# Softmax of the first attention on ScalarE head by head, its tiles spread over the state recurrence, and the write term of the state chain added in the copy

## The chip, the core and the metric

The kernel runs on one core of one Trainium2 chip. The metric is device time of one execution in microseconds (us): the median of three runs before is 4936.85 us (4933.53 to 4939.53). Below, PE is TensorE, DVE is VectorE, ACT is ScalarE, POOL is GpSimd and SP is SyncE, whose queue issues the DMAs. Each engine works through its own instructions strictly in order.

## What is computed

The program is a stack of four blocks: an attention with a recurrent memory (called the first attention here), a six-layer local-attention model, a linear attention, and a two-layer local-attention model, each behind a modulated layer norm. Only the first attention is touched. Its reference, cut to what matters (B=4, T=512 in its own set-up; the kernel is called with 2 sequences of 2048 tokens, 16 heads of 8 dimensions, chunks of 64 tokens):

```python
def t_step(M, kv):
    k_t, v_t = kv
    Mk = jnp.einsum('bhde,bhe->bhd', M, k_t)
    forget = Mk[..., :, None] * k_t[..., None, :]
    write = v_t[..., :, None] * k_t[..., None, :]
    return (M - alpha * forget + beta * write, None)

def chunk_step(M, qkv):
    qi, ki, vi = qkv
    scores = jnp.einsum('bhid,bhjd->bhij', qi, ki) * scale
    scores = jnp.where(mask, -jnp.inf, scores)
    attn = jax.nn.softmax(scores, axis=-1)
    attn_out = jnp.einsum('bhij,bhjd->bhid', attn, vi)
    mem_out = jnp.einsum('bhid,bhde->bhie', qi, M)
    chunk_out = attn_out + 0.1 * mem_out
    M, _ = jax.lax.scan(t_step, M, kv)      # 64 steps
    return (M, chunk_out)
_, outs = jax.lax.scan(chunk_step, M0, (qc_all, kc_all, vc_all))   # 32 chunks
```

So every chunk has a causal softmax attention inside itself, and a 8x8 memory per head that is carried from chunk to chunk.

## The kernel before

The first attention is `l0_attention`. Its instruction order is written out by hand (`manual_schedule`): what the program emits first stands first on each engine, with semaphores put in by the framework where data, buffers or PSUM banks need them.

**Tiles.** The 4096 tokens make 32 tiles of 128 tokens (2 chunks). A tile's softmax weights are 128 rows x 16 heads x 64 keys: 1024 numbers per partition. The heads are split in two halves q of 8 heads, 512 numbers each, one PSUM bank per half. For one tile i:

- `spread(i)` (L390): POOL lays the keys out as block rows `kx`.
- `scores(i)` (L400): PE writes the causal mask (L405) and the scores (L411) into `ps_s`, one buffer of two banks.
- `shifted(i)` (L418): DVE takes the maximum of every row and head (L422), subtracts it (L424, PSUM to SBUF tile `sm`); ACT takes the exponential of all 1024 numbers at once (L425).
- `weights(i)` (L427): DVE sums them (L430) and takes the reciprocal (L431), POOL multiplies (L432).
- `keys_first(i)` (L434): PE transposes the weights (L440), ACT copies them out as `pT` (L444).
- `values(i)` (L446): PE projects the values into `ps_o` (L450), ACT copies them to `vbd` (L457).
- `mix(i, c)` (L462): PE multiplies weights and values for chunk c (L469), into the same banks of `ps_o`; ACT copies the result to `hT` (L476).

**The recurrence.** The memory's transition over a chunk does not depend on the memory itself, so all 64 chunks advance together: `step(t)` (L360) is called 64 times, each four DVE instructions (L366, L367, L369, L371) that depend on each other, and after every fourth step one ACT copy (L375). When the 64 steps are done, `products_done` sends the products through DRAM (`prd`) to lay them out anew.

**The chain over chunks.** Then `chain(n)` runs for n = 0 to 31, one after the other, for both sequences. PE multiplies the transition with the memory (L552) and adds the write term `rm` by a matmul with the identity into the same PSUM range (L557); DVE copies the sum out as the new memory `mn` (two copies of 64 partitions, L563); PE multiplies the old memory with the output weights (L567), and ACT copies that out as `xs` (L572, shown in the trace under the buffer name `bx`). `transitions(g)` prepares 8 chunks (L516, L530, L537), `turn_writes` turns the write terms (L498, L502), and `finish(g)` (`out_`, `centre`, `variance`, `scale`, L579 to L630) writes the output and the next layer norm for 1024 tokens.

**The main loop** (L675 to L699) weaves both. Iteration i emits `keys_first(i)`, `weights(i+1)`, `scores(i+2)`, `spread(i+3)`, `values(i+1)`, `shifted(i+2)`, `mix(i, 0)`, `mix(i, 1)`, and between them seven calls of `slot(i, part)`, which emit as many entries of the list `todo` as are due: 64 steps and `products_done` first (65 entries), then another 65: turning, transitions, chains and finishing. Which entries fall due when is one line (L670): the first 65 are spread over the tiles 0 to 25, the others over the tiles 26 to 31:

```python
due = 5 * q // 14 if i < 26 else 65 + (len(todo) - 65) * (q - 182) // 42
```

After the loop, `finish(3)` runs by itself, and the local models (`local_models`, untouched) start.

Of the kernel before, what the change touches and what calls it, by code (L numbers as in the profile page):

```python
# [72 lines left out]
def tile_kernel(ctx: ExitStack, tc: tile.TileContext, a: dict, out: bass.AP):  # L73
    nc = tc.nc
# [37 lines left out]
    identb = const.tile([128, 128], BF16, name="identb")  # L112
# [75 lines left out]
    def l0_attention(m):  # L188
# [17 lines left out]
        maskb = cp.tile([128, 8, 64], BF16, name="maskb")  # L206
# [22 lines left out]
        with tc.tile_pool(name="a_p", bufs=2) as wp, tc.tile_pool(  # L229
            name="a_psP", bufs=2, space=PSUM  # L230
# [101 lines left out]
        wk = ctx2.enter_context(tc.tile_pool(name="a_w", bufs=2))  # L332
        psS = ctx2.enter_context(tc.tile_pool(name="a_psS", bufs=1, space=PSUM))
# [26 lines left out]
        def step(t):  # L360
            full = (128, 8, 8, 8)
            kt = bc(kd[:, t].unsqueeze(2), full)
            four = zks[:, t // 4 % 2]
            zk = four[:, t % 4]
            tm = wk.tile([128, 8, 8, 8], F32, name="tm")
            nc.vector.tensor_tensor(tm, z, kt, ALU.mult)  # L366
            nc.vector.tensor_reduce(zk, tm, AX.X, ALU.add)  # L367
            up = wk.tile([128, 8, 8, 8], F32, name="up")
            nc.vector.tensor_tensor(up, bc(zk.unsqueeze(3), full), kt, ALU.mult)  # L369
            flat = lambda v: v.rearrange("p c r e -> p (c r e)")  # L370
            nc.vector.scalar_tensor_tensor(  # L371
                flat(z), flat(up), na[:, 0:1], flat(z), ALU.mult, ALU.add
            )
            if t % 4 == 0:
                nc.scalar.copy(  # L375
                    wr[:, :, :, t:t + 4], four.rearrange("p t c r -> p r c t")
                )
# [3 lines left out]
        for i in range(2):  # L381

            v = wk.tile([128, 2, 8, 72], F32, name=f"vbd{i}", bufs=1)
# [15 lines left out]

        def scores(i):  # L400
            t0 = 128 * order[i]
            kx = L[i].pop("kx")
            sp = L[i]["s"] = psS.tile([128, 1024], F32, name="ps_s")
            for q in range(2):
                nc.tensor.matmul(  # L405
                    sp[:, 512 * q:512 * q + 512], lhsT=identb,
                    rhs=maskb.rearrange("p h k -> p (h k)"), start=True, stop=False,
                )
            for c in range(2):
                for q in range(2):  # L410
                    nc.tensor.matmul(  # L411
                        sp[64 * c:64 * c + 64, 512 * q:512 * q + 512],
                        lhsT=qT[64 * q:64 * q + 64, t0 + 64 * c:t0 + 64 * c + 64],
                        rhs=kx[64 * q:64 * q + 64, c].rearrange("p h j -> p (h j)"),
                        start=False, stop=True,
                    )

        def shifted(i):  # L418

            v = L[i].pop("s").rearrange("p (q h k) -> p h q k", q=2, h=8)  # L420
            mx = wk.tile([128, 8, 2], F32, name="mx")
            nc.vector.tensor_reduce(mx, v, AX.X, ALU.max)  # L422
            sm = L[i]["p"] = wk.tile([128, 8, 2, 64], F32, name="sm", bufs=3)
            nc.vector.tensor_tensor(sm, v, bc(mx.unsqueeze(3), (128, 8, 2, 64)), ALU.subtract)  # L424
            nc.scalar.activation(sm, sm, AF.Exp)  # L425

        def weights(i):  # L427
            sm = L[i]["p"]
            rs = wk.tile([128, 8, 2], F32, name="rs")
            nc.vector.tensor_reduce(rs, sm, AX.X, ALU.add)  # L430
            nc.vector.reciprocal(rs, rs)  # L431
            nc.gpsimd.tensor_tensor(sm, sm, bc(rs.unsqueeze(3), (128, 8, 2, 64)), ALU.mult)  # L432

# [28 lines left out]
        def mix(i, c):  # L462
            t0 = 128 * order[i]
            vf = vbd[i % 2].rearrange("p c h x -> p c (h x)")
            pT = L[i]["pT"]
            for h in range(8):
                for q in range(2):
                    qs = slice(64 * q, 64 * q + 64)
                    nc.tensor.matmul(  # L469
                        po[qs, q, 0, i % 2, 64 * c:64 * c + 64],  # L470
                        lhsT=vf[qs, c, 64 * h:64 * h + 64],
                        rhs=pT[qs, h, 64 * c:64 * c + 64], start=(h == 0), stop=(h == 7),
                    )
# [6 lines left out]
        E = {}  # L480
        QS = [slice(0, 64), slice(64, 128)]
# [61 lines left out]
        def chain(n):  # L543
            c = n % 8
            pm = E["p"][:, :, 128 * (n % 2):128 * (n % 2) + 128].rearrange(
                "p q (b f) -> p q b f", b=2)
            px = E["p"][:, :, 256:512].rearrange("p q (b f) -> p q b f", b=2)
            if n < 31:
                for b in range(B):
                    for q in range(2):  # L550
                        if n:
                            nc.tensor.matmul(  # L552
                                pm[QS[q], q, b], lhsT=E["bd"][QS[q], b, c],
                                rhs=E["m"][QS[q], b], start=True, stop=False,
                            )
                    for q in range(2):
                        nc.tensor.matmul(  # L557
                            pm[QS[q], q, b], lhsT=ident[QS[q], QS[q]],
                            rhs=E["rm"][QS[q], c % 2, b, c // 2], start=(n == 0), stop=True,
                        )  # L560
                mn = wk.tile([128, 2, 64], F32, name="mn")
                for q in range(2):
                    nc.vector.tensor_copy(mn[QS[q]], pm[QS[q], q])  # L563
            if n:
                for b in range(B):
                    for q in range(2):
                        nc.tensor.matmul(  # L567
                            px[QS[q], q, b], lhsT=E["m"][QS[q], b], rhs=wo10[QS[q], :],
                            start=True, stop=True,
                        )  # L570
                for q in range(2):
                    nc.scalar.copy(E["xs"][QS[q], :, c, :], px[QS[q], q])  # L572
            if n < 31:
                E["m"] = mn
# [58 lines left out]
        def finish(g):  # L633
            bs = (g, NBLK + g)
            return [lambda f=f, k=k: f(k) for f in (out_, centre, variance, scale) for k in bs]
# [11 lines left out]
        todo = [lambda t=t: step(t) for t in reversed(range(64))]  # L647
# [16 lines left out]
        def slot(i, part):  # L664

            nonlocal done
            if i < 0:
                return
            q = 7 * i + part + 1
            due = 5 * q // 14 if i < 26 else 65 + (len(todo) - 65) * (q - 182) // 42  # L670
            while done < due:
                todo[done]()
                done += 1

        for i in range(-3, NT):  # L675
            if i >= 0:
                keys_first(i)
            if 0 <= i + 1 < NT:
                weights(i + 1)
            slot(i, 0)  # L680
            if 0 <= i + 2 < NT:
                scores(i + 2)
            slot(i, 1)
            if i + 3 < NT:
                spread(i + 3)
            if 0 <= i + 1 < NT:
                values(i + 1)
            slot(i, 2)
            if 0 <= i + 2 < NT:
                shifted(i + 2)  # L690
            slot(i, 3)
            if i >= 0:
                mix(i, 0)
                slot(i, 4)
                mix(i, 1)
            slot(i, 5)
            slot(i, 6)
            if i == -1:
                regroup()  # L699
# [843 lines left out]
    with ExitStack() as ctx2:  # L1543
        hs0 = l0_attention(m0)
# [65 lines left out]
```

## Time and profile before

| What | us |
|---|---|
| median of the three runs | 4936.85 |
| the profiled execution's own time | 4928.13 |
| its span (first to last instruction) | 4926.3 |
| PE busy in the span | 4493.8 (91%) |
| DVE busy in the span | 3949.1 (80%) |
| POOL busy | 2781.2 (56%) |
| ACT busy | 2637.9 (54%) |

How to read it: a share of busy time is a mean over stages with different limits. The first attention takes only the first part of the span: its tile loop begins at about 87 us, the last of the 64 steps starts at 381.9 us, the last chain matmul stands at about 550 us, and the first matmul of the local models (L871) at 566.6 us. The page's 40 slices are 123 us each, so the tile loop lies in slices 1 to 5; there PE shows 5 to 7 tenths and DVE 8 to 9 tenths in the slices that hold the steps. Everything after 566.6 us belongs to parts that the diff does not touch.

### The profile page before, as it was taken

The page shows a single profiled execution, that of the slowest core. Times are in us where ns is not written, and L with a number is a line of the kernel's source. Part 1 is how long each engine was busy: PE and PEld are TensorE (multiplying, and loading weights), DVE is VectorE, ACT ScalarE, POOL GpSimd, SP SyncE. Part 2 cuts the span into 40 slices and gives each one's busy share as a digit, 9 for nine tenths or more (in the row PEclk, how much of TensorE's full clock was granted, in tenths as well). Part 3 has the DMA queues.
Part 4 walks back from the last instruction along what each step waited for, and adds up shares of the span by engine and source line. Part 5 has one row for each costly group of instructions (what it writes and reads, how often), then busy time and mean ns, then how long its engine had stood idle before and what let it go on. Part 6 is the DMA issues. An engine that isn't in the chain of part 4 may idle for free.

```text
span 4926.3 us, 166334 instructions
## 1 busy us (share of the span) xinstructions
PE 4493.8 (91%) x73028; PEld 3066.5 (62%) x73058; DVE 3949.1 (80%) x6840; ACT 2637.9 (54%) x4207; POOL 2781.2 (56%) x1666
## 2 busy tenths in 40 slices
PE   5667799999999999999999999999999998899997
PEld 4445566666666666666666666666666665556554
DVE  6994488888888888888887888888877777788886
ACT  3223355555555555555555555555555555465554
POOL 3332366666666666666666666666655544455552
PEclk8778899999999999999999999999999999999999
DMA  2000222222222322223222322222212111111121
GB/s 78 1 1 25 85 65 67 69 73 70 69 65 64 87 68 65 66 73 76 68 64 64 79 72 65 66 74 69 68 51 59 50 51 46 37 46 49 51 58 41
DMA packets 222468, 295.31 MB, mean 60 GB/s; under 512 B 75657, under 2 KB 95409, under 8 KB 221745
## 3 DMA queue, kind: packets, MB, share of 16 engines
q1 hardware_dynamic: 221744, 284.67, 22.4%
q8 instruction: 576, 9.44, 0.8%
q14 instruction: 148, 1.20, 0.1%
HBM read 40.98 MB, written 10.75 MB: 10 GB/s over the span
## 4 chain that ended last, share of the span: by engine, by line
PE 49%; DVE 25%; ACT 7%; POOL 5%; issue 3%; DMA 0%; SPq 0%; POOLq 0%; DVEq 0%; ACTq 0%
PE ps_qk L871 12%; PE ps_o L1050 5%; PE ps_v L957 5%; DVE ps_qk L899 5%; PE ps_f L1150 5%; DVE t L888 5%; PE ps_turn L938 4%; PE ps_y L1067 4%; POOL r L894 4%; PE ps_s L997 3%; DVE r L883 3%; PE ps_fy L1175 3%; ACT sq L873 2%; DVE rs L1021 2%; PE ps_pT L1032 2%
## 5 line engine op out<-in xcount | busy, mean ns | idle before, releaser
L894 POOL TENSOR_TENSOR r<-r,t 128x1024 f32<-128x1024 f32 x448 | 1060.2, 2367 | 911.8 <-DVE t L888 794.3
L906 POOL TENSOR_TENSOR r<-r,rq_y 128x1024 f32<-128x1024 f32 x448 | 843.8, 1902 | 517.9 <-DVE rq_y L180 495.8
L873 ACT ACTIVATE sq<-ps_qk 128x1024 f32<-128x1024 f32 x448 | 460.6, 1028 | 1082.3 <-PE ps_qk L871 1014.7
L871 PE MATMUL ps_qk<-wp,hs 128*128 128x512 f32 x1792 | 893.8, 621 | 105.7 <-DVE rq_y L180 77.1
L883 DVE TENSOR_TENSOR r<-ps_qk,tb 128x1024 f32<-128x1024 f32 (+1 forms) x512 | 550.7, 1076 | 211.8 <-ACT sq L873 198.4
L1050 PEld LDWEIGHTS ps_o<-pT,v 64*64 64x64 f32 (+1 forms) x26624 | 479.4, 136 | 304.5 <-ACT pT L1033 160.9
L888 DVE TENSOR_TENSOR t<-ps_qk,tb 128x1024 f32<-128x1024 f32 (+1 forms) x512 | 554.1, 1082 | 143.1 <-POOL r L894 142.4
L1023 POOL TENSOR_TENSOR sm<-sm,rs 128x1024 f32<-128x1024 f32 x256 | 487.5, 1904 | 210.2 <-DVE rs L1022 126.9
L1050 PE MATMUL ps_o<-pT,v 64*64 64x32 f32 (+1 forms) x26624 | 531.2, 221 | 37.0 <-ACT pT L1033 19.2
L899 DVE TENSOR_REDUCE ps_qk<-sq 128x16 f32<-128x1024 f32 x448 | 549.0, 1226 | 11.9
L871 PEld LDWEIGHTS ps_qk<-wp,hs 128*128 128x128 f32 x1792 | 310.1, 193 | 364.3 <-issue 236.1
L938 PEld LDWEIGHTS ps_turn<-ident,r 128*128 128x128 f32 x3584 | 411.7, 143 | 125.2 <-issue 99.4
L957 PE MATMUL ps_v<-wp,hs 128*128 128x512 f32 x896 | 481.9, 639 | 1.0 <-ACT oT L1056 0.8
L1067 PEld LDWEIGHTS ps_y<-oT,wo 128*128 128x128 f32 x3584 | 430.2, 193 | 46.9 <-issue 42.5
L938 PE MATMUL ps_turn<-ident,r 128*128 128x128 f32 x3584 | 447.3, 277 | 9.7 <-POOL r L906 4.1
L1067 PE MATMUL ps_y<-oT,wo 128*128 128x128 f32 x3584 | 446.3, 276 | 1.5 <-ACT oT L1056 1.5
L1056 ACT COPY oT<-ps_o 128x512 f32<-128x512 f32 x448 | 244.0, 588 | 281.9 <-PE ps_o L1050 281.2
L1005 DVE TENSOR_REDUCE mx<-ps_s 128x16 f32<-128x1024 f32 (+1 forms) x256 | 312.5, 1221 | 97.4 <-PE ps_s L997 95.6
L997 PE MATMUL ps_s<-kT,qT 64*32 64x64 f32 (+1 forms) x26624 | 377.9, 230 | 0.7 <-issue 0.5
L997 PEld LDWEIGHTS ps_s<-kT,qT 64*32 64x32 f32 (+1 forms) x26624 | 325.8, 107 | 63.7 <-issue 53.0
L1150 PE MATMUL ps_f<-fx,w 128*128 128x512 f32 (+1 forms) x768 | 356.1, 600 | 2.5 <-DVE fx L1133 1.7
L1021 DVE TENSOR_REDUCE rs<-sm 128x16 f32<-128x1024 f32 (+1 forms) x256 | 310.5, 1213 | 51.1 <-ACT sm L1014 49.0
(265 smaller groups left out, 6850.5 us busy)
## 6 DMA issues: line engine op xcount, KB each, us to landing
v<-vn SPq DMA_DIRECT2D x1276, 128.0 KB
v<-vn SPq DMA_DIRECT2D x744, 64.0 KB
v<-vn SPq DMA_DIRECT2D x64, 256.0 KB
wp<-in_L_ffn_Wqkv SPq DMA_DIRECT2D x20, 512.0 KB
xD<-xb SPq DMA_DIRECT2D x24, 256.0 KB
xb<-xD SPq DMA_DIRECT2D x24, 256.0 KB
cs<-in_cos SPq DMA_DIRECT2D x128, 32.0 KB
cs<-in_sin SPq DMA_DIRECT2D x128, 32.0 KB
```

Of the source, the lines that this page charges most:

```text
L871: nc.tensor.matmul(pq[:, js], lhsT=hw, rhs=wts[g, u][:, js], start=True, stop=True)
L883: nc.vector.tensor_tensor(r[:, es].rearrange("p (h d) -> p h d", d=DH), pq[:, es].rearrange("p (h d) -> p h d", d=DH), bc(tb[:, 0, s].unsq ...
L888: nc.vector.tensor_tensor(t2[:, es].rearrange("p (h s d) -> p h s d", s=2, d=32), pq[:, es].rearrange("p (h s d) -> p h s d", s=2, d=32)[: ...
L894: nc.gpsimd.tensor_tensor(r, r, t2, ALU.add)
L899: nc.vector.tensor_reduce(pq[:, 16 * v:16 * v + 16], st[i].pop(("sq", v)).rearrange("p (h d) -> p h d", d=DH), AX.X, ALU.add,)
L906: nc.gpsimd.tensor_tensor(rv, rv, bc(y[:, 16 * v:16 * v + 16].unsqueeze(2), (128, 16, DH)), ALU.mult)
L938: nc.tensor.transpose(p[:, c * 128:(c + 1) * 128], r[:, cs], ident)
L957: nc.tensor.matmul(p, lhsT=hw, rhs=wv, start=True, stop=True)
L997: nc.tensor.matmul(sp[W * w:W * w + W, c0:c0 + 2 * W], lhsT=qT[64 * q:64 * q + 64, cc, W * w:W * w + W], rhs=kT[64 * q:64 * q + 64, cc, W ...
L1050: nc.tensor.matmul(po[s][64 * q:64 * q + 64, 128 * c + W * w:128 * c + W * w + W], lhsT=v2[kp, w, co:co + 64], rhs=pT[kp, q, c, W * w:W * ...
L1067: nc.tensor.matmul(py[:, 0:128], lhsT=wts[g, "o"][:, c * NO + s, :], rhs=oT[:, s, c, :], start=(c + s == 0), stop=(c == 3 and s == NO - 1),)
L1150: nc.tensor.matmul(ps_[c][0:sz], lhsT=wts[g, "w1"][:, o:o + sz], rhs=S["x"], start=True, stop=True,)
```

## The change

Four edits, all in `l0_attention`:

1. The scores' PSUM tile is split into two, one bank per half q, and the three matmuls of a half stand together.
2. `shifted` is replaced by `maxima` (two DVE maximum reductions of 512 numbers, negated) and `exps(i, q)`: eight ACT exponentials of 64 numbers for each half, straight from PSUM, with the negated maximum as the bias and the sum over the 64 numbers returned through the accumulator (`accum_out`) into `rs`. The subtraction on DVE (L424) and the sum on DVE (L430) are gone.
3. In the main loop `maxima(i+2)` and `exps(i+2, 0)` stand where `shifted(i+2)` stood, `exps(i+2, 1)` after `mix(i, 1)`. The first 65 entries of `todo` are spread over tiles 0 to 28, the other 65 over tiles 29 to 31.
4. In `chain` the identity matmuls (L557) are gone; the DVE copy that makes `mn` becomes an addition of PSUM and `rm`.

```diff
         def scores(i):
...
             for q in range(2):
+                sp = L[i]["s", q] = psS.tile([128, 8, 64], F32, name=f"ps_s{q}")
+                flat = sp.rearrange("p h k -> p (h k)")
                 nc.tensor.matmul(
-                    sp[:, 512 * q:512 * q + 512], lhsT=identb,
+                    flat, lhsT=identb, rhs=maskb.rearrange("p h k -> p (h k)"),
...
-        def shifted(i):
...
-            nc.vector.tensor_reduce(mx, v, AX.X, ALU.max)
-            sm = L[i]["p"] = wk.tile([128, 8, 2, 64], F32, name="sm", bufs=3)
-            nc.vector.tensor_tensor(sm, v, bc(mx.unsqueeze(3), (128, 8, 2, 64)), ALU.subtract)
-            nc.scalar.activation(sm, sm, AF.Exp)
+        def maxima(i):
+            mx = L[i]["mx"] = wk.tile([128, 8, 2], F32, name="mx")
+            for q in range(2):
+                nc.vector.tensor_reduce(mx[:, :, q], L[i]["s", q], AX.X, ALU.max, negate=True)
+
+        def exps(i, q):
...
+            sp, mx = L[i].pop(("s", q)), L[i]["mx"]
+            for h in range(8):
+                nc.scalar.activation(
+                    L[i]["p"][:, h, q, :], sp[:, h, :], AF.Exp, bias=mx[:, h, q:q + 1],
+                    accum_out=L[i]["rs"][:, h, q:q + 1],
+                )
 
         def weights(i):
-            sm = L[i]["p"]
-            rs = wk.tile([128, 8, 2], F32, name="rs")
-            nc.vector.tensor_reduce(rs, sm, AX.X, ALU.add)
+            sm, rs = L[i]["p"], L[i].pop("rs")
             nc.vector.reciprocal(rs, rs)
...
-                                rhs=E["m"][QS[q], b], start=True, stop=False,
+                                rhs=E["m"][QS[q], b], start=True, stop=True,
                             )
-                    for q in range(2):
-                        nc.tensor.matmul(
-                            pm[QS[q], q, b], lhsT=ident[QS[q], QS[q]],
-                            rhs=E["rm"][QS[q], c % 2, b, c // 2], start=(n == 0), stop=True,
-                        )
...
-                    nc.vector.tensor_copy(mn[QS[q]], pm[QS[q], q])
+                    r = E["rm"][QS[q], c % 2, :, c // 2]
+                    if n:
+                        nc.vector.tensor_tensor(mn[QS[q]], pm[QS[q], q], r, ALU.add)
+                    else:
+                        nc.vector.tensor_copy(mn[QS[q]], r)
...
-            due = 5 * q // 14 if i < 26 else 65 + (len(todo) - 65) * (q - 182) // 42
+            due = 65 * q // 203 if i < 29 else 65 + (len(todo) - 65) * (q - 203) // 21
...
-                shifted(i + 2)
+                maxima(i + 2)
+                exps(i + 2, 0)
             slot(i, 3)
             if i >= 0:
                 mix(i, 0)
                 slot(i, 4)
                 mix(i, 1)
+            if 0 <= i + 2 < NT:
+                exps(i + 2, 1)
```

More of the change, by code (lines that the diff above doesn't have):

```diff
@@ L402, in scores @@
             kx = L[i].pop("kx")
-            sp = L[i]["s"] = psS.tile([128, 1024], F32, name="ps_s")
             for q in range(2):
+                sp = L[i]["s", q] = psS.tile([128, 8, 64], F32, name=f"ps_s{q}")
+                flat = sp.rearrange("p h k -> p (h k)")
                 nc.tensor.matmul(
-                    sp[:, 512 * q:512 * q + 512], lhsT=identb,
-                    rhs=maskb.rearrange("p h k -> p (h k)"), start=True, stop=False,
-                )
-            for c in range(2):
-                for q in range(2):
+                    flat, lhsT=identb, rhs=maskb.rearrange("p h k -> p (h k)"),
+                    start=True, stop=False,
+                )
+                for c in range(2):
                     nc.tensor.matmul(
-                        sp[64 * c:64 * c + 64, 512 * q:512 * q + 512],
+                        flat[64 * c:64 * c + 64, :],
                         lhsT=qT[64 * q:64 * q + 64, t0 + 64 * c:t0 + 64 * c + 64],
@@ L416, in scores @@
                     )
-        def shifted(i):
-            v = L[i].pop("s").rearrange("p (q h k) -> p h q k", q=2, h=8)
-            mx = wk.tile([128, 8, 2], F32, name="mx")
-            nc.vector.tensor_reduce(mx, v, AX.X, ALU.max)
-            sm = L[i]["p"] = wk.tile([128, 8, 2, 64], F32, name="sm", bufs=3)
-            nc.vector.tensor_tensor(sm, v, bc(mx.unsqueeze(3), (128, 8, 2, 64)), ALU.subtract)
-            nc.scalar.activation(sm, sm, AF.Exp)
+        def maxima(i):
[3 more added lines that the diff above has]
+        def exps(i, q):
+            if q == 0:
+                L[i]["p"] = wk.tile([128, 8, 2, 64], F32, name="sm", bufs=3)
+                L[i]["rs"] = wk.tile([128, 8, 2], F32, name="rs")
+            sp, mx = L[i].pop(("s", q)), L[i]["mx"]
[4 more added lines that the diff above has]
+                )
         def weights(i):
-            sm = L[i]["p"]
-            rs = wk.tile([128, 8, 2], F32, name="rs")
-            nc.vector.tensor_reduce(rs, sm, AX.X, ALU.add)
+            sm, rs = L[i]["p"], L[i].pop("rs")
             nc.vector.reciprocal(rs, rs)
@@ L553, in chain @@
                                 pm[QS[q], q, b], lhsT=E["bd"][QS[q], b, c],
-                                rhs=E["m"][QS[q], b], start=True, stop=False,
+                                rhs=E["m"][QS[q], b], start=True, stop=True,
                             )
-                    for q in range(2):
-                        nc.tensor.matmul(
-                            pm[QS[q], q, b], lhsT=ident[QS[q], QS[q]],
-                            rhs=E["rm"][QS[q], c % 2, b, c // 2], start=(n == 0), stop=True,
-                        )
                 mn = wk.tile([128, 2, 64], F32, name="mn")
                 for q in range(2):
-                    nc.vector.tensor_copy(mn[QS[q]], pm[QS[q], q])
+                    r = E["rm"][QS[q], c % 2, :, c // 2]
[3 more added lines that the diff above has]
+                        nc.vector.tensor_copy(mn[QS[q]], r)
             if n:
```

## The prediction

> **What bounds the kernel now.** I first took the time line to place the tile loop, then the busy time by stretch. In the answer the columns are the stretch, its length, busy time of PE, PEld, DVE, ACT and POOL with instruction counts, granted clock, DMA share and GB/s.
>
> ```profile
> 102.40:384.80 282.40, 175.28 (x2325) 119.27 (x2349) 272.18 (x361) 89.08 (x200) 101.50 (x54) 0.76 0.00 1
> 384.80:553.00 168.20, 128.55 (x1740) 100.52 (x1740) 53.11 (x115) 57.23 (x128) 29.37 (x22) 0.86 0.08 25
> ```
>
> The first stretch holds tiles 0 to 25 and the 64 steps: DVE is busy 272 of 282 us, everyone else below two thirds. The second holds tiles 26 to 31 and the chains: PE leads with 129 of 168 us, DVE has 53. So one edit can pay in each stretch, and by a different engine. The groups by form show what a tile puts on DVE (last numbers: busy, mean ns | idle before).
>
> ```profile
> L371 DVE SCALAR_TENSOR_TENSOR z<-up,c_L_attn_a,z 128x512 f32<-128x512 f32 x64 | 48.4, 756 | 2.2
> L367 DVE TENSOR_REDUCE zks<-tm 128x64 f32<-128x512 f32 x64 | 44.5, 695 | 3.2
> L424 DVE TENSOR_TENSOR sm<-ps_s,mx 128x1024 f32<-128x1024 f32 x32 | 39.2, 1224 | 1.1
> L422 DVE TENSOR_REDUCE mx<-ps_s 128x16 f32<-128x1024 f32 x32 | 39.0, 1219 | 4.9 <-PE ps_s L411 4.8
> L430 DVE TENSOR_REDUCE rs<-sm 128x16 f32<-128x1024 f32 x32 | 38.8, 1214 | 2.4 <-ACT sm L425 2.4
> L431 DVE RECIPROCAL rs<-rs 128x16 f32<-128x16 f32 x32 | 8.1, 253 | 1.1
> ```
>
> A tile costs DVE 1.22 + 1.22 + 1.21 + 0.25 = 3.91 us. A step, from its start at 201.42 us to the next instruction's at 204.20, takes 2.78. With 64/26 = 2.46 steps a tile that is 10.75, against 282.4/26 = 10.86 measured: DVE is the bound, with no wait worth naming. For what ACT pays per small instruction I read its groups and one run of three in the time line (start, length):
>
> ```profile
> L444 ACT COPY pT<-ps_pT 128x512 f32<-128x512 f32 x64 | 35.0, 590 | 6.5 <-PE ps_pT L440 5.8
> L457 ACT COPY vbd<-ps_o 64x128 f32<-64x128 f32 x64 | 16.7, 261 | 12.6 <-PE ps_o L450 11.7
> L1160 ACT ACTIVATE u<-ps_f,c 128x512 f32<-128x512 f32 x128 | 82.1, 685 | 19.4 <-PE ps_f L1150 18.8
> L200 ACT ACTIVATE c_L_attn_a<-c_L_attn_a 128x1 f32<-128x1 f32 x1 | 0.2, 203 | 2.5 <-DMA c_L_attn_a<-in_L_attn_a 2.5
> 766.75 1.83 ACT L1160 ACTIVATE u<-ps_f,c 128x512 f32<-128x512 f32 x3
> ```
>
> Three activations with a bias column, 685 ns each, end within 1.83 us: one starts every (1.83 - 0.685)/2 = 0.57 us, an overlap of 0.11.
>
> **Part 1, exponential on ACT.** DVE loses L424 and L430 and has two maxima of 512 for one of 1024: 2 x 0.69 (L367's size) for 1.22. A tile falls from 3.91 to 1.63, and with 64/29 = 2.21 steps DVE's own work is 1.63 + 6.14 = 7.8 us.
>
> ACT gets 16 pairs of a 64-number exponential and an accumulator read for one 1.06 us exponential. The exponential: an element costs (590 - 261)/384 = 0.857 ns, so 448 fewer than L1160's take 0.38 off 0.57: 0.19 us start to start. The read has no row. Below: 0, if it hides in the exponential. Above: 0.203, ACT's smallest instruction (L200) unoverlapped, behind an exponential that doesn't overlap either (0.685 - 0.38 = 0.30): 0.50 a pair. I take the small instruction with the usual overlap, 0.203 - 0.11 = 0.09, as ACT's queue overlaps wherever no semaphore stands between, and none does here. A pair is 0.285, 16 are 4.56; the ends are 3.0 and 8.1.
>
> The Trainium skill speaks against sixteen small activations: "ScalarE: Activation LUTs", section "What ACT_TABLE_LOAD costs", gives 280 ns + 0.833 per element with a pointer bias and an overlap of 93, hence an estimate of 0.24 for 64 numbers where this trace's spacing gives 0.19; the sum below would be 16 x 0.05 x 29 = 23 us longer by it.
>
> ACT's total, 4.56 plus copies (two of 0.59, four of 0.26, 0.55 x 0.37 for L375: 2.4) is 7.0 us a tile, below DVE. But the two engines now wait for each other in a ring. The reciprocal of tile i+2 on DVE, at the head of the next iteration, waits for the last pair of `exps(i+2, 1)`; behind it are queued that iteration's steps and maxima. `exps` in turn waits for the maxima. One turn:
> - DVE from the last pair: semaphore 0.06, reciprocal 0.2, the one step that falls due in slots 0 to 2 (steps are 3.12 slots apart), 2.78, first maximum 0.69, semaphore 0.06: 3.8 us. Beside it PE does half 1's scores (L411, about 1.5) and the values (0.5), ACT `pT` (1.07) and `vbd` (0.55), some 3.2 us: hidden, with 0.6 to spare.
> - then ACT: 16 pairs 4.56, `hT` copies 0.56, last read's tail and semaphore 0.15, share of L375 0.1: 5.4 us. PE's mix (2.1 us at full clock, 3.6 at half) lies beside the first half. DVE does the second maximum and 1.25 steps here, 4 us, but where two steps fall due (28% of tiles) 6.1 us: mean 5.6.
>
> Turn: 9.4 us, with DVE idle some 1.6 of it. 29 tiles: 271 us. It starts later: tile 1's exponentials and the `kd` copies queue on ACT ahead of the first step: about 104 instead of 102.4, plus 1.9 as the `kd` copies (2 x 1.97) delay tile 0's `exps`. End of the steps: 104 + 1.9 + 271 = 377 instead of 384.8: **-8 us**, with three more tiles done.
>
> **Part 2, tail.** These groups of PE are from 385 to 553 us:
>
> ```profile
> L567 PE MATMUL ps_n<-wo,mn 64*64 64x128 f32 x248 | 23.6, 317 | 29.9 <-DVE mn L563 28.7 <-ACT bx L572 1.2
> L552 PE MATMUL ps_n<-mn,bx 64*64 64x64 f32 x240 | 18.6, 245 | 5.7 <-ACT bx L572 5.3 <-POOL bx L516 0.4
> L557 PE MATMUL ps_n<-rm,ident 64*64 64x64 f32 x248 | 18.2, 236 | 0.0
> L469 PE MATMUL ps_o<-pT,vbd 64*64 64x64 f32 x384 | 16.5, 242 | 0.0
> ```
>
> PE's in-order queue is the path: its busy 129 us and about 36 of waits, mostly 0.9 us behind every `mn` copy, make up the 168. Three tiles leave: 3 mixes of 16.5/6, 3 transposes of 8.2/5 (L440), 2 scores of 1.8 (L405 and L411), 3 values of 0.46: about **-18**. DVE loses some 14 us of tile work here, of which little stood ahead of an `mn`: -3. Covers that go: chains with nothing between them wait on the `xs` copy (0.9 us; L552 shows 5.3 in all). Some 11 such gaps instead of 6: +5. Tile 31's two blocks of 2.3 us on ACT stand in front of `xs` copies, where before four of 1.06 did: +2. `products_done` (8 DMAs, then the load of `pc`) moves from tile 25's end to tile 28's on SP, which is idle in both; the 12 us from there to the first L552 (384.8 to 397.06) were filled by turning, `rm`, scores and a mix, and lose part of that: +1. The 0.37 us ACT copies, POOL's `spread` and the output's loads keep their places.
>
> **Part 3, write term in the copy.** The two identity groups between L552's lie about 0.12 us each at full clock, 0.21 at half (535.08 us on): 0.24 to 0.42 x 31 = 7.4 to 13 us, on the path since `mn` waits for them. Adding from PSUM and SBUF is priced by L1073, the same shape (64x128): 286 ns, as L563's copy: nothing. I take **-8**, near the full-clock end, as the granted clock of that stretch is 0.86; `rm` comes from DVE itself and is ready long before.
>
> Tail: -18 - 3 + 5 + 2 + 1 - 8 = -21; I take **-19**, as PE's granted clock (0.86) may fall with more gaps. Sum: -8 - 19 = -27. On the profiled execution, 4928.13 us (span 4926.3, 1.8 around it), that is 4901; this one lay 8.7 below the median, so on 4936.85 it is **4910 us**.
>
> **Rivals.** *The read waits for its exponential.* If the accumulator can only be read when the exponential has drained, a pair costs 0.19 + 0.203 = 0.39, 16 are 6.3, the ring turns in 3.8 + 7.1 = 10.9 us and 29 tiles take 316: 45 more than I count, 4955 us, slower. It decides from 0.375 a pair upward; 0.35 is break-even (27/29 = 0.9 us a tile over 5.6). For it: every L425 waits on DVE at present, so ACT has shown no dependent pair back to back; L457's pairs, which wait by semaphore, don't overlap (0.55 for two). Against it: pairs carry no semaphore.
>
> *The read is free.* At 0.19 a pair ACT's part is 3.9, with the two-step tiles 4.5 in the mean, the turn 8.3, 29 tiles 240: 4879 us. DVE's 7.8 is the floor.
>
> *The tail does not shrink.* Chains keep their latency (matmul, copy, matmul, copy: about 2.9 us x 32 = 93), the output's loads their 3.2 us, so that what the three tiles leave turns into waits for `xs` and `mn`. Then only part 1 remains: 4929 us, no change. For it: 30 us of PE's idle before L567. Against: PE is busy 129 of 168.
>
> **How the numbers follow.** Forecast 0.48, its own range 4896 to 4926; slow read 0.25; free read 0.12; tail unchanged 0.15. A measurement here can tell about 0.2%, 10 us. Faster: 0.48 + 0.12 and a little of the third, 0.62; same 0.15; slower 0.23. Range 4879 to 4956: to the free read below and past the slow read above, leaving out the pair at 0.50 (12.7 us a turn, 5006).
>
> **What would show it.** Pairs on ACT 0.285 us apart; DVE idle about 1.6 us a tile in front of the reciprocal, released by ACT; tiles 9.4 us apart; the steps' end near 377 us; the tail some 149 us long, with L552 waiting more on `xs`. I am wrong if a pair takes over 0.35, if the steps' stretch shows ACT waiting for PE's scores, or if PE's idle in the tail grows by what its work shrinks.

## The result and the profile after

| | before | after |
|---|---|---|
| median, us | 4937.17 (8 runs, 4931.15 to 4940.96) | 4954.58 (8 runs, 4945.79 to 4959.94) |
| ratio after/before, 95% | | 1.0035 [1.0025, 1.0045] |
| profiled execution, us | 4928.13 | 4947.9 |
| its span | 4926.3 | 4946.1 |

The changed kernel is slower by 17.4 us. It was predicted faster by 27. The page's own line of busy time shows little of why:

```profile
PE 4547.7 (92%) x72809; PEld 3088.3 (62%) x72810; DVE 3876.8 (78%) x6808; ACT 2757.0 (56%) x5199; POOL 2780.7 (56%) x1666
```

DVE lost 72 us and ACT gained 119, as meant. But PE gained 54 us although the diff gives it fewer matmuls: 47.8 of them in the stretch of the steps, 6.4 in the tail. Busy time by stretch shows it. The columns are those of the prediction: stretch, length, busy time of PE, PEld, DVE, ACT and POOL, PE's granted clock, DMA share, GB/s. The first stretch runs to the end of the 64 steps (start of the copy `zs`). The second, the tail, runs from there to the first matmul of the local models, which need the whole of this attention. First the tail of the kernel before, with that boundary:

```profile
384.90:566.80 181.90, 139.80 (x1803) 110.03 (x1803) 57.02 (x123) 59.04 (x130) 31.39 (x24) 0.86 0.12 37
```

Then both stretches of the kernel after:

```profile
105.00:390.00 285.00, 220.56 (x2610) 137.14 (x2609) 216.48 (x343) 211.01 (x1144) 111.39 (x60) 0.81 0.01 2
390.00:579.40 189.40, 146.20 (x1295) 112.12 (x1295) 44.07 (x110) 54.38 (x143) 20.11 (x18) 0.68 0.11 35
```

In the stretch of the steps PE had 172.8 us in the kernel before (105 to 384.9 us); now there are three tiles more, and the scores take longer. Their rows, before and after:

```profile
L411 PE MATMUL ps_s<-kx,qT 64*64 64x512 f32 x212 | 40.1, 834 | 5.8 <-issue 3.5
L411 PE MATMUL ps_s<-kx,qT 64*64 64x512 f32 x232 | 71.1, 693 | 0.0
```

A tile's scores took 40.1/26.5 = 1.51 us and take 71.1/29 = 2.45. The kernel before emitted the matmuls of the two halves in turn, and its records overlap (212 of 834 ns in 40.1 us, 4.4 at a time); edit 1 puts each half by itself, and 2.3 overlap.

Three more things are to be seen. The steps end at 390.0 instead of 384.9 us: DVE is now busy 216 of 285 us, so it is no longer full, and ACT has 211. The tail is 7.5 us longer (189.4 against 181.9), with 508 fewer matmul records in it. And PE's busy time in the tail rose by 6.4 us, while its idle time is as before (43.2 against 42.1). So the lost time is in the matmuls themselves: the granted clock fell from 0.86 to 0.68. A *link* below is one call `chain(n)`: first product (transition times memory), copy `mn` on DVE, second product (memory times output weights), copy `xs` on ACT. The groups of PE in the tail of the kernel after, up to the last link (390 to 563 us; busy, mean ns of one | idle before), answer to those that the prediction showed:

```profile
L573 PE MATMUL ps_n<-wo,mn 64*64 64x128 f32 x248 | 29.1, 373 | 30.2 <-DVE mn L567 29.0 <-ACT bx L578 1.2
L559 PE MATMUL ps_n<-mn,bx 64*64 64x64 f32 x240 | 17.5, 280 | 8.6 <-ACT bx L578 7.2 <-DVE mn L569 1.5
L476 PE MATMUL ps_o<-pT,vbd 64*64 64x64 f32 x192 | 10.2, 280 | 0.0
```

A matmul of the second product takes 373 ns where it took 317 (L567 before), one of the first 280 instead of 245 (L552), one of the mix 280 instead of 242 (L469). The waits for `mn` are the same 29 us.

Of the 19.8 us between the two spans, 5.1 lie in the steps, 7.5 in the tail and 7.2 behind it, in code that the diff does not touch. That last part took 4350.8 to 4375.9 us in the thirteen single executions profiled here, in no order that follows the edits. It is left out of the reading below.

### The profile page after: what moved, and what is told of

It is laid out like the page before. It is cut to its first block, busy times and chain, and to the rows that moved or that the text cites. A ratio compares the mean times of both kernels' runs of the same rounds, so it can differ in the third digit from the quotient of the medians.

```text
span 4946.1 us, 166815 instructions
## 1 busy us (share of the span) xinstructions
PE 4547.7 (92%) x72809; PEld 3088.3 (62%) x72810; DVE 3876.8 (78%) x6808; ACT 2757.0 (56%) x5199; POOL 2780.7 (56%) x1666
## 4 chain that ended last, share of the span: by engine, by line
PE 49%; DVE 25%; ACT 7%; POOL 5%; issue 3%; DMA 1%; SPq 0%; POOLq 0%; DVEq 0%; ACTq 0%
PE ps_qk L880 12%; PE ps_o L1059 6%; PE ps_v L966 5%; DVE ps_qk L908 5%; DVE t L897 5%; PE ps_f L1159 5%; PE ps_turn L947 4%; PE ps_y L1076 4%; POOL r L903 4%; PE ps_s L1006 3%; DVE r L892 3%; PE ps_fy L1184 3%; ACT sq L882 2%; DVE rs L1030 2%; PE ps_pT L1041 2%
```

## The experiments

Each is an edit of the kernel after, unless it says otherwise. One table holds what all profiles show. "Steps end" and "tail" are as above, and the clocks are PE's granted clock in the two stretches. The ratio is to the kernel before on the same chip; the medians come from several chips, so rows are compared by their ratios.

| kernel | steps end, us | clock | tail, us | clock | median, us | ratio [95%] |
|---|---|---|---|---|---|---|
| before | 384.9 | 0.76 | 181.9 | 0.86 | 4937.17 | |
| after | 390.0 | 0.81 | 189.4 | 0.68 | 4954.58 | 1.0035 [1.0025, 1.0045] |
| e1_identity_back | 389.1 | 0.82 | 191.9 | 0.71 | 4936.54 | 1.0017 [1.0006, 1.0027] |
| e2_old_spread | 363.4 | 0.80 | 205.3 | 0.73 | 4933.08 | 1.0008 [0.9999, 1.0018] |
| e3_filler | 388.9 | 0.81 | 170.4 | 0.81 | 4930.28 | 0.9999 [0.9986, 1.0011] |
| e4_join_only | 384.1 | 0.75 | 189.0 | 0.75 | 4939.38 | 1.0020 [1.0008, 1.0032] |
| e5_recip_late | 355.3 | 0.90 | 188.0 | 0.68 | 4918.68 | 0.9974 [0.9960, 0.9989] |
| e6_values_first | 359.8 | 0.87 | 196.2 | 0.64 | 4927.41 | 0.9992 [0.9979, 1.0005] |
| e7_values_first_filler | 358.4 | 0.88 | 167.9 | 0.83 | 4895.15 | 0.9939 [0.9924, 0.9955] |
| e8_own_bank | 355.4 | 0.89 | 157.3 | 0.82 | 4884.61 | 0.9917 [0.9898, 0.9936] |
| e9_small_filler | 386.6 | 0.83 | 194.1 | 0.66 | 4950.27 | 1.0033 [1.0016, 1.0051] |
| e10_best | 357.1 | 0.88 | 157.7 | 0.81 | 4882.10 | 0.9903 [0.9887, 0.9918] |
| e11_more_filler | 360.9 | 0.88 | 165.8 | 0.81 | 4896.48 | 0.9929 [0.9915, 0.9943] |

A theory was to explain the tail: with work gone, PE pauses more often, its granted clock falls, and what is left gets slower (CLOCK). The rival: the chain's latency sets the tail and the joined copy or the waits cost it (LATENCY or WORK in the expectations).

**The write term alone, on the kernel before.** Only edit 4 of the change is made:

```diff
-   rhs=E["m"][QS[q], b], start=True, stop=False,
+   rhs=E["m"][QS[q], b], start=True, stop=True,
...
-   for q in range(2):
-       nc.tensor.matmul(
-           pm[QS[q], q, b], lhsT=ident[QS[q], QS[q]],
-           rhs=E["rm"][QS[q], c % 2, b, c // 2], start=(n == 0), stop=True,
-       )
...
-   nc.vector.tensor_copy(mn[QS[q]], pm[QS[q], q])
+   r = E["rm"][QS[q], c % 2, :, c // 2]
+   if n:
+       nc.vector.tensor_tensor(mn[QS[q]], pm[QS[q], q], r, ALU.add)
...
```

> The kernel before with the write term joined in the copy and nothing else. By the prediction's step (identity matmuls on the path, 0.24 us a chain): 8 us faster than before, 4929. Theory CLOCK: less activity in the tail lowers the granted clock there below 0.86 and gives part of it back: 4930 to 4942 us.

Its tail by stretch:

```profile
384.10:573.10 189.00, 146.60 (x1552) 114.50 (x1556) 58.59 (x123) 59.35 (x130) 31.38 (x24) 0.75 0.12 35
```

251 matmul records are gone, yet PE is busy 146.6 us instead of 139.8, the clock is 0.75 instead of 0.86 and the tail is 7.1 us longer. A single execution tells less than that: the tails of the kernel after, e5 and e6, whose chains are the same, lie between 188.0 and 196.2. But the median of ten executions is slower too, by 0.20% with an interval of 0.08 to 0.32%, where the prediction had counted 8 us gained. Taking this work from PE did not make the kernel faster.

**The write term back as a matmul, in the kernel after.** The reverse edit:

```diff
-   rhs=E["m"][QS[q], b], start=True, stop=True,
+   rhs=E["m"][QS[q], b], start=True, stop=False,
...
+   for q in range(2):
+       nc.tensor.matmul(pm[QS[q], q, b], lhsT=ident[QS[q], QS[q]],
+           rhs=E["rm"][QS[q], c % 2, b, c // 2], start=(n == 0), stop=True)
...
-       nc.vector.tensor_tensor(mn[QS[q]], pm[QS[q], q], r, ALU.add)
...
+   nc.vector.tensor_copy(mn[QS[q]], pm[QS[q], q])
```

> The changed kernel with the identity matmuls of the chain put back and the plain copy restored. Theory CLOCK (the tail is long because PE, with three tiles and the identity matmuls gone, is granted a lower clock, 0.66 instead of 0.86): the 248 extra matmuls raise the activity, the granted clock between the end of the steps and the local models goes above 0.70 and the time is equal or lower than the changed kernel's (4945 to 4957 us). Rival LATENCY (the tail is a fixed chain of waits, and every matmul on it counts): 7 to 13 us slower than the changed kernel, 4962 to 4968, clock unchanged.

The tail is 2.5 us longer and its clock 0.71 instead of 0.68; the ratio is 1.0017 instead of 1.0035, with intervals that overlap a little. So some 250 matmuls more cost nothing that can be measured. The clock recovers little, though: in this tail, with three tiles out of it, the same matmuls that went with 0.86 before do not bring it back.

**The old spread over tiles.** The first 65 entries go over tiles 0 to 25 again:

```diff
-   due = 65 * q // 203 if i < 29 else 65 + (len(todo) - 65) * (q - 203) // 21
+   due = 5 * q // 14 if i < 26 else 65 + (len(todo) - 65) * (q - 182) // 42
```

> The changed kernel with the old due times: 64 steps over tiles 0 to 25, the rest over tiles 26 to 31. Theory CLOCK: with six tiles' PE work in it the tail's granted clock returns towards 0.85 and the tail (end of the steps to the first matmul of the local models) takes some 175 us, 14 less than the changed kernel's 189, though it holds three more tiles; the steps' stretch takes 26 tiles of about 9.9 us. Together 4915 to 4930 us. Rival LATENCY or WORK: three more tiles cost the tail what they cost before, it becomes 200 us or more and the time is 4945 to 4960.

The steps end 26.6 us earlier and the tail is 15.9 us longer: moving three tiles beside the steps cost 10.7 us more than it brought, and the medians agree (1.0008 against 1.0035). The clock of its tail, 0.73, is not the 0.85 that CLOCK expected: with six tiles but without the identity matmuls it is near e4's 0.75. Against e4 the difference is the whole new softmax: the exponentials on ACT with their new places, and the scores half by half (edit 1). Together they lengthen a tail of six tiles by 16.3 us. PE's idle has 5.0 of that and its busy time 11.3, at about the same clock; the scores alone (L411) take 12.3 us there for four tiles, where e4's take 4.8 for three. The way from the tail before to the tail after, in single executions, is thus + 7.1 (joined write, e4 against before), + 16.3 (new softmax, e2 against e4), - 15.9 (three tiles out, after against e2).

**Matmuls for nothing.** In the 19 links n = 12 to 30, three matmuls whose result nobody reads stand between the first product and the second, where PE waits for `mn`:

```diff
             if n < 31:
...
+            if n >= 12 and n < 31:
+                if "fill" not in E:
+                    E["fill"] = psS.tile([128, 8, 64], F32, name="ps_s0")
+                for _ in range(3):
+                    nc.tensor.matmul(
+                        E["fill"].rearrange("p h k -> p (h k)"), lhsT=identb,
+                        rhs=maskb.rearrange("p h k -> p (h k)"), start=True, stop=True)
```

> The changed kernel with three bf16 matmuls of 128x512 (mask and identity, result never read) put into PE's wait for the memory's copy in chains 12 to 30. They add work only, in a gap of about 0.75 us. Theory CLOCK: granted clock in the tail's second two thirds goes from 0.6 to 0.7 to above 0.85, the tail becomes 10 to 18 us shorter, 4936 to 4945 us. Rival LATENCY: PE's filler lengthens each chain by up to 0.5 us, 19 chains, time 4955 to 4965.

Its control has the same number of matmuls at the same places, with 16 columns instead of 512 (`E["fill"][:, 0, 0:16]`, `maskb[:, 0, 0:16]`):

> The control of e3_filler: the same three matmuls at the same places, but 16 columns wide instead of 512, so that PE works hardly longer. Theory CLOCK (it is PE's activity that counts): the granted clock in the tail stays near 0.68 and the tail near 189 us, time as the changed kernel's. Rival ORDER (the inserted instructions help by delaying or parting what stands behind them, not by their work): the tail falls to about 170 us as with e3.

The two tails, first with 512 columns:

```profile
388.90:559.30 170.40, 135.10 (x1342) 96.64 (x1353) 44.06 (x109) 53.80 (x142) 20.11 (x18) 0.81 0.13 41
```

and with 16:

```profile
386.60:580.70 194.10, 154.66 (x1351) 118.89 (x1352) 44.12 (x110) 54.47 (x143) 20.11 (x18) 0.66 0.11 33
```

The fillers themselves, first of e3, then of e9:

```profile
L574 PE MATMUL ps_s<-maskb,identb 128*128 128x512 bf16 x47 | 13.8, 392 | 1.8 <-issue 1.8
```

```profile
L574 PE MATMUL ps_s<-maskb,identb 128*128 128x16 bf16 x57 | 4.6, 178 | 0.0
```

Without its fillers PE has 135.1 - 13.8 = 121 us of work in the tail of e3 (10 of 57 filler records are missing, so somewhat less), and 154.7 - 4.6 = 150 in that of e9. It is the same work. The long fillers raise the clock from 0.68 to 0.81 and take 19 us off the tail; the short ones do neither. So it is PE's activity and not a changed order of the queue. The links show it one by one. Link 20 in the kernel after (start, length, engine, line), both products:

```profile
500.64 0.69 PE L559 MATMUL ps_n<-mn,bx 64*64 64x64 f32 x8
502.07 1.12 PE L573 MATMUL ps_n<-wo,mn 64*64 64x128 f32 x8 [0.75 <-DVE mn L567]
```

and the same link in e3:

```profile
496.19 0.45 PE L559 MATMUL ps_n<-mn,bx 64*64 64x64 f32 x8
496.80 0.59 PE L574 MATMUL ps_s<-maskb,identb 128*128 128x512 bf16 x2 [0.16 <-issue]
497.39 0.65 PE L581 MATMUL ps_n<-wo,mn 64*64 64x128 f32 x8
```

The eight matmuls of a second product take either some 0.65 us or some 1.12, and little between. How many of a kernel's 31 second products took over 1 us:

| kernel | links 1 to 11 | links 12 to 31 |
|---|---|---|
| before | 2 of 11 | 5 of 20 |
| e4_join_only | 7 | 6 |
| after | 9 | 10 |
| e1_identity_back | 7 | 7 |
| e9_small_filler | 9 | 9 |
| e3_filler | 10 | 2 |
| e7_values_first_filler | 8 | 2 |
| e10_best | 9 | 1 |
| e11_more_filler | 9 | 1 |

Up to link 11, where no kernel has fillers, those with long fillers are as slow as the kernel after; from there on they alone run at the short length, in all links but link 12 itself and, in two kernels, link 24. The medians (1.0035 and 0.9999, some 18 us apart) agree with the 19.

**The ring of DVE and ACT.** A second question was the stretch of the steps, 13 us longer than predicted. One theory: the reciprocal at the head of an iteration holds DVE until ACT's last pair (RING). The rival: PE's scores and values, late at low clock, hold ACT (PE-PATH). The first is tried by moving `weights(i+1)` behind the first half's exponentials:

```diff
-            if 0 <= i + 1 < NT:
-                weights(i + 1)
             slot(i, 0)
...
                 exps(i + 2, 0)
+            if 0 <= i + 1 < NT:
+                weights(i + 1)
             slot(i, 3)
```

> The changed kernel with the reciprocal (and POOL's multiplication) of tile i+1 emitted after the maxima of tile i+2 instead of at the head of the iteration. Theory RING (DVE and ACT wait for each other because the reciprocal blocks the next steps until the last exponential is done): DVE's idle before the reciprocal (60.8 us in all) goes, a tile takes 8.6 to 9.2 us instead of 9.7, the steps' stretch is 15 to 30 us shorter, 4925 to 4940 us on the changed kernel's scale of 4954. Rival PE-PATH (PE's scores, values and mix at a low clock set the tile's time, ACT waiting for vbd and hT): the tile stays at 9.5 to 9.8 us.

The second, on top of that, by emitting the values ahead of the scores:

```diff
             slot(i, 0)
+            if 0 <= i + 1 < NT:
+                values(i + 1)
             if 0 <= i + 2 < NT:
                 scores(i + 2)
...
-            if 0 <= i + 1 < NT:
-                values(i + 1)
             slot(i, 2)
```

> As e5_recip_late, and the values' matmuls (with vbd's copies) emitted before the scores of tile i+2. Theory RING: like e5 to within 5 us. Rival PE-PATH: only here the tile falls clearly, to 8.0 to 8.8 us, as the first half's exponentials no longer wait for scores and values at a low clock; 30 to 45 us less than the changed kernel.

The reciprocal's group in the stretch of the steps, in the kernel after:

```profile
L438 DVE RECIPROCAL rs<-rs 128x16 f32<-128x16 f32 x29 | 7.3, 253 | 57.6 <-ACT sm L431 55.1 <-ACT wr L375 2.5
```

In e5, with the maxima:

```profile
L421 DVE TENSOR_REDUCE mx<-ps_s 128x8 f32<-128x512 f32 x58 | 38.4, 685 | 19.8 <-PE ps_s L411 19.8
L438 DVE RECIPROCAL rs<-rs 128x16 f32<-128x16 f32 x29 | 7.0, 243 | 0.0
```

57.6 us of DVE's idle before the reciprocal are gone, 19.8 come back before the maxima, and the steps end 34.7 us earlier (1.2 us a tile). In e6 the wait of the copy `vbd` on the values all but disappears (31.8 us in the kernel after; in e6 the line below), but the steps end no earlier than in e5 (359.8 against 355.3), and the median is not better. ACT waits elsewhere instead, 28.2 us for the maxima. PE-PATH's clear fall did not come, and the steps' end is within RING's 5 us of e5's. So the reciprocal's place was the bound, and the values were not a second one.

```profile
L464 ACT COPY vbd<-ps_o 64x128 f32<-64x128 f32 x58 | 15.8, 273 | 0.7
```

**Both cures together, and the bank of the second product.** e7 is e6 with the fillers.

> e6_values_first with the filler matmuls of e3_filler in chains 12 to 30. Theory CLOCK: the filler takes another 17 to 20 us off the tail (189 to about 170 us), whatever the steps' stretch does; ratio to the kernel before 0.990 to 0.996.

The two gains add: 0.9939, with the tail at 167.9. What is left in its chains is a wait that the data don't ask for. The second product multiplies the old memory, which is ready, yet the program's semaphores hold it on PE until DVE has read the first product out as `mn`: both products lie in one PSUM tile. e8 is e7 with the second product in a tile of its own from n = 12 on:

```diff
+            if n >= 12:
+                if "px" not in E:
+                    E["px"] = psS.tile([128, 8, 64], F32, name="ps_s1")
+                px = E["px"].rearrange("p (q b f) k -> p q b (f k)", q=2, b=2)
```

> e7 with the output product of chains 12 to 30 in the PSUM bank that the scores' second half has left, instead of in the banks of the memory, so that the next chain's matmuls don't wait for the xs copy. If the xs wait is on the path, 0.9 us for some of 19 chains: 5 to 12 us less than e7 in the tail. If the chains' interleaved work hides it: within 3 us of e7.

The second product's group in the tail of e7, up to its last links:

```profile
L581 PE MATMUL ps_n<-wo,mn 64*64 64x128 f32 x246 | 24.9, 331 | 18.9 <-DVE mn L567 17.4 <-ACT bx L586 1.2
```

and its two groups in that of e8, first the links from n = 12 on, then those before:

```profile
L585 PE MATMUL ps_s<-wo,mn 64*64 64x128 f32 x160 | 13.5, 289 | 2.6 <-ACT bx L590 2.6
L585 PE MATMUL ps_n<-wo,mn 64*64 64x128 f32 x88 | 11.4, 405 | 11.0 <-DVE mn L571 11.0
```

In its own tile the product no longer waits for `mn` at all; the 11.0 us that remain are the old links. The expectation had looked to the next link's wait for `xs` instead. Of the waits of both products, those for `mn` fall by 6.4 us and those for `xs` by 1.6. The tail loses 10.6 us, and the medians (4895.15 and 4884.61) 10.5, with intervals that overlap. The tails with three fillers are 170.4 and 167.9 us without the tile of its own (e3, e7), 157.3 and 157.7 with it (e8, e10). e10 is e5 (the values stay where they were) with the fillers and the own tile, and e11 is e10 with five fillers a link for three:

> e5_recip_late (values left where the changed kernel has them) with the filler and the separate bank of e8. If the three edits add up as their stages showed (steps' end at 355 us, tail 157 us): 4 us less or more than e8, ratio to the kernel before 0.989 to 0.993.

> e10 with five filler matmuls a chain instead of three. Theory CLOCK with saturation: the granted clock in the tail rises a little (0.82 to 0.85 or more), but five matmuls are 1.1 us at full clock, longer than the 0.75 us gap, and lengthen 19 chains by 0.3 us each: within 6 us of e10.

e10 beats both kernels: 4882.10 us, 0.9903 [0.9887, 0.9918] of the kernel before. Against the kernel after it ends the steps 32.9 us earlier and has 31.7 us less tail, 64.6 in all; the ratios (0.9903 and 1.0035 of 4931) differ by 65 us. Five fillers are 8.1 us worse in the tail at the same clock of 0.81, and the median is 14 us worse, where the expectation was a higher clock and a time within 6 us. With three, the second products from link 13 on all have the short length already (1 of 20 is long in both), so more fillers had nothing to raise there; PE's busy time grows by 10.3 us. They outlast the gap they fill, as it seems, and the chain pays for the rest.

## Why the prediction was wrong, step by step

**Direction and size.** 4954.58 us lies inside the range (4879 to 4956), but at its slow end and on the wrong side of the kernel before. The number is that of the rival with the slow read (4955), by coincidence: its mechanism did not happen. In the profiled executions the steps end 13 us later than predicted and the tail is 26.5 us longer (+7.5 for -19); what is behind the tail was counted as unchanged.

**The pair on ACT: right.** One half of a tile in the time line of the kernel after:

```profile
200.98 0.31 ACT L431 ACTIVATE sm<-ps_s,mx 128x64 f32<-128x64 f32 x1 [2.24 <-DVE mx L421]
201.19 0.19 ACT L431 ACTIVATION_READ_ACCUMULATOR sm<-ps_s,mx 128x1 f32 x1
201.29 0.30 ACT L431 ACTIVATE sm<-ps_s,mx 128x64 f32<-128x64 f32 x1
201.48 0.20 ACT L431 ACTIVATION_READ_ACCUMULATOR sm<-ps_s,mx 128x1 f32 x1
201.58 0.31 ACT L431 ACTIVATE sm<-ps_s,mx 128x64 f32<-128x64 f32 x1
```

The exponentials start 0.29 to 0.31 us apart against 0.285 predicted. The read starts 0.1 us before its exponential's record ends, and 0.10 after its own start the next exponential begins: both parts overlap as taken (0.19 and 0.09). Both the slow read (0.39) and the free one (0.19) are out. The page "ScalarE: Activation LUTs" of the Trainium skill, section "What ACT_TABLE_LOAD costs", made the exponential alone 0.24 as an estimate; the spacing from an exponential to its read is 0.19 to 0.21 here.

**The ring: there, but under-sized.** DVE stands idle before the reciprocal, released by ACT, for 57.6/29 = 2.0 us a tile (1.6 predicted). The first reciprocal of the ring starts at 108.3 us, not at 104: 4.3 late. From there 29 turns take 390.0 - 108.3 - 1.9 (for the `kd` copies) = 279.8 us, 9.65 each, instead of 271, which makes 8.8. So the steps end at 390.0 instead of 377, and "-8" became +5. What the step had wrong is the cover "PE's mix (2.1 us at full clock, 3.6 at half) lies beside the first half", a cover that was to cost nothing. ACT's wait for the mix over the stretch:

```profile
L483 ACT COPY hT<-ps_o 64x128 f32<-64x128 f32 x58 | 15.2, 262 | 9.8 <-PE ps_o L476 9.4
```

One turn of the kernel after, in the time line, from a reciprocal on:

```profile
206.43 0.25 DVE L438 RECIPROCAL rs<-rs 128x16 f32<-128x16 f32 x1 [2.10 <-ACT sm L431]
206.89 1.97 PE L411 MATMUL ps_s<-kx,qT 64*64 64x512 f32 x4
208.79 0.69 PE L457 MATMUL ps_o<-c_L_attn_wT,hT 128*64 128x64 f32 x8
209.59 0.54 ACT L464 COPY vbd<-ps_o 64x128 f32<-64x128 f32 x2 [2.30 <-PE ps_o L457]
210.19 3.43 PE L476 MATMUL ps_o<-pT,vbd 64*64 64x64 f32 x64 [0.69 <-ACT vbd L464]
213.67 0.53 ACT L483 COPY hT<-ps_o 64x128 f32<-64x128 f32 x2 [0.55 <-PE ps_o L476]
```

and the next:

```profile
216.78 0.25 DVE L438 RECIPROCAL rs<-rs 128x16 f32<-128x16 f32 x1 [3.27 <-ACT sm L431]
217.04 1.07 PE L411 MATMUL ps_s<-kx,qT 64*64 64x512 f32 x4
218.04 0.45 PE L457 MATMUL ps_o<-c_L_attn_wT,hT 128*64 128x64 f32 x8
219.19 2.08 PE L476 MATMUL ps_o<-pT,vbd 64*64 64x64 f32 x64 [0.70 <-ACT vbd L464]
222.84 0.27 ACT L483 COPY hT<-ps_o 64x128 f32<-64x128 f32 x1
```

In the second PE has its full clock: scores, values and mix take 3.6 us together, the copies `hT` stand 6.06 us behind the reciprocal, right behind the first half's eight pairs, and the turn is 9.19 us long. In the first the same three take 6.1 us, one after the other with ACT's copy between, `hT` stands 7.24 us behind the reciprocal, and the turn is 10.35 (0.55 us of the difference is the wait for the mix, and the rest the copy L375 of every fourth step, which stands ahead of `hT` in this turn). The mix at half clock had been laid beside the first half, but behind scores and values at full clock. The 28 turns after the first bear it out. In 13 the mix takes 2.08 us, and they last 9.16 us in the mean, as the prediction's 3.8 + 5.4 without its two-step tiles. In 15 it takes 3.3 to 3.7 us, and they last 10.06; six of these hold three steps, and the other nine, with two as the 13 have, last 9.91. So here too the clock of PE, low in some turns, was the missing term. Up to the first exponential both turns need 3.73 us, as DVE's side was counted (3.8).

**Three tiles leave the tail, "-18": about right.** The kernel after against e2 gives -15.9, with the clock 0.05 lower. But the three tiles cost 26.6 us beside the steps, so that the move itself loses 10.7; the prediction had this cost inside its ring (3 x 9.4 = 28) and never set the two numbers side by side.

**ACT's work in the tail, "+5" and "+2": under-sized.** The new softmax costs a tail of six tiles 16.3 us (e4 against e2). Part of that is a term that the prediction did not have: the scores of edit 1, half by half, 3.1 us of PE a tile there instead of 1.6. What all this costs a tail of three was not measured by itself.

**The identity matmuls, "-8", and the 2 us for the clock: the step that failed.** "On the path since `mn` waits for them" holds, and they were priced at the granted clock of the kernel before, 0.86. But that clock was not a constant of the stretch: it followed PE's activity. With the identity matmuls alone removed it was 0.75, the tail 7.1 us longer and the median 0.20% slower (e4); with fewer tiles beside the chains it was 0.68. Putting them back there cost nothing (e1), so -8 is not there in either kernel. The prediction saw the danger ("as PE's granted clock (0.86) may fall with more gaps") and gave it 2 us of its -21; raising the clock to 0.81 by work that nobody needs brought 19 (e3). So the tail was to lose 19 us and gained 7.5.

**What was named as a sign of error.** "PE's idle in the tail grows by what its work shrinks" did not come: idle stayed at 43 us. The rival "the tail does not shrink" was right in its outcome and wrong in its cause. ACT waiting behind PE's scores and values did come (31.1 us before `vbd`), but taking that wait away did not end the steps earlier (e6 against e5).

**Left open.** Nothing here tells from which activity on the clock falls, nor why the untouched rest differs by up to 25 us between single executions. The exponential on ACT without the other edits was not run, nor edit 1 alone, so the share of the longer scores in the 17.4 us is open.

## What to carry to other kernels

Where a latency-bound chain of small matmuls stands alone on PE, matmuls are not priced by their own time: look at the granted clock of the stretch first, and ask whether what is removed keeps it up. Work that fills a wait on another engine can be worth more than its absence, as long as it is shorter than the wait. Before an instruction is moved to another engine, look for the first instruction that waits for it in an in-order queue: here one reciprocal of 0.25 us, standing a few places too early, held 35 us.

## What the runs showed of the hardware

- The share of busy time does not tell the granted clock, as a matmul at low clock is busy for longer: PE is busy 0.77 of the tail before (clock 0.86), 0.77 after (0.68), 0.79 in e3 (0.81) and 0.80 in e9 (0.66). 57 matmuls of 512 columns spread over 19 links raise it, 57 of 16 columns do not. Within a stretch the same eight matmuls take 0.65 or 1.12 us; by this, a mean clock between is a mixture of the two.
- The longest of PE's waits on another engine in the tail after was 3.0 us, and most of those for `mn` some 0.75. The Trainium skill, "TensorE: Matmul & The Clock Gate", section "HAM oscillation — how this bites in real kernels", warns of idle gaps over about 3.4 us; none of that length shows among these waits, and the clock fell all the same. Its section "A second HAM failure mode: psum-queue depth-cycling" tells of another kernel (bf16, 512 columns), where frequent short pauses between groups of matmuls make the clock swing between two states; the links here, at 0.65 or 1.12 us, look like that.
- The sum of an activation comes as an instruction of its own, ACTIVATION_READ_ACCUMULATOR, 217 ns by its record, of which about 0.1 us remain up to the next exponential.
- The eight score matmuls of a tile took 1.09 us where the two halves came in turn (at 185.38 us in the kernel before), and four of one half alone take 1.07 (at 217.04 us in the kernel after): what overlapped before follows one another now.
- In this program, of two products in one PSUM tile the second waits until DVE has read the first, although it needs none of its data; a tile of its own for 20 links made the tail 10.6 us shorter (e8 against e7).
